# A sandwich of attention and feed-forward layers: MLPs of the state-space stage started in earlier turns, and work moved across the stage's two borders

## The chip, the core and the metric

The kernel runs on one core of one Trainium2 chip. Five engines take part: TensorE (PE, with its weight loads shown apart as PEld), VectorE (DVE), ScalarE (ACT), GpSimd (POOL) and SyncE (SP, which issues the transfers). Each engine works through its own list of instructions in the order in which the program gave them; they meet through semaphores. The metric is the device time of one execution in microseconds (us), and of several runs the median.

## The reference

Four pairs of an attention-like and a feed-forward layer work on one tensor of 16 sequences of 256 positions and 128 channels. Each layer's input is normalized, its output too, and added:

```python
x = x + _layernorm(_L2_attn_ref(_layernorm(x, axis=-1), ...), axis=-1)
x = x + _layernorm(_L2_ffn_ref(_layernorm(x, axis=-1), w1, b1, w2, b2), axis=-1)
x = x + _layernorm(_L3_attn_ref(_layernorm(x, axis=-1), ...), axis=-1)
```

The change lies in the last of these and at its two borders. `_L2_ffn_ref` is a plain MLP, `gelu(x @ w1 + b1) @ w2 + b2` with 512 hidden units. `_L3_attn_ref` is long. Cut to its skeleton, with x0 its normalized input:

```python
xm = mix_m[0] * x + mix_m[1] * x0                     # x is x0 here
n = rms_norm(xm)
value, gate = split(n @ in_proj_w)                    # value goes through a convolution of 4 taps and silu
y = selective_scan(value, A, xm @ B_proj_w, xm @ C_proj_w, dt) + D_param * value
xm = xm + mamba_scale * (y * silu(gate) @ out_proj_w)
xm = xm + m_mlp_scale * (square(relu(rms_norm(xm) @ m_fc_w)) @ m_proj_w)
xa = mix_a[0] * xm + mix_a[1] * x0                    # "the mix"
q, k, v = projections of rms_norm(xa), q and k normalized and rotated
xa = xa + attn_scale * (softmax(q k^T, causal) v @ o_w)      # 16 heads of 8
```

## The kernel before

The 4096 rows are held as eight groups (`NG`), each 512 rows: a tile of 128 partitions by 4 by 128 channels. The kernel is a sequence of stages. Each stage opens a pool of work buffers and of PSUM banks and closes them at its end, so the first tiles of a stage wait until the last instruction of the stage before it has finished with the memory.

Three stages matter here: `stage_l2_attn` (attention of the third pair), `stage_trunk` (MLP of the third pair, scan and MLP of the fourth), and `l3_gqa` (attention of the fourth pair).

Inside these stages the order of the work is written out by hand. `Ctx.turns` takes a list of generators with the turn in which each starts. In each turn it goes through the list in its order and lets each generator that has started do one step, up to its next `yield` (up to three steps if it is behind). What is issued in a turn goes to the engines' lists in that order, and no scheduler moves it afterwards.

`stage_trunk` has four kinds of generators. For each group g, `before(g)` does the whole MLP of the third pair (`l2_ffn`), then the statistics of the result, the first mix into `xm[g]`, and the values and gates of the scan (`l3_values`). `l3_scan` does the scan's 14 steps. `behind(g)` does the second MLP (`l3_mid_mlp`), and after it the mix: x is normalized again by the kept statistics, multiplied on POOL (L1685), `xm` multiplied on DVE (L1687) and the sum taken on POOL (L1688). `rotate` prepares the rotated queries and keys of group 0 for the attention. Their turns are

```python
at = [23 + 8 * g for g in range(NG)]
items = [(at[g] - 2, l3_scan(k, g, xm[g], w, lm, got[g])) for g in range(NG)]
items += [(at[g] + 12, behind(g)) for g in range(NG)]
items += [(at[g] - 23, before(g)) for g in range(NG)][::-1]
```

Thus a group enters every 8 turns; `before(g)` takes 24 turns, the scan of g starts at turn 21 + 8g and ends 14 turns later, when `behind(g)` starts.

Some buffers are few: `mlp_h`, the hidden layer, has one; `y` has two and serves the MLP's output as well as both mixes; `n` and `nT` have three.

`attention_stage` runs the two attentions. It first lets the generator `head` of group 0 do `first` steps, then calls `attention_pools`, which fills the value tiles `at_vm` and `at_pc` on POOL (L363, L368) and makes three small casts on DVE (L375), then finishes `head(0)`. This stretch lies ahead of the hand-written turns. After it, twelve turns belong to each group; heads of later groups start `early` turns ahead, and one more generator, `beside`, may be given, which starts at turn 9. In `head`, the steps up to the third make the transposed keys `kT`, the fourth the queries `qT`, the fifth `km`: `variants` (L382 on ACT and L383 on POOL) multiplies the keys by four masks, so that heads can be told apart in one product. `qm` follows likewise from the queries.

Names that a reader meets below: `k.stats` is L255 and L257 on DVE and a scaling and a power on POOL (L244, L245); `k.normed` is L264 on DVE, four instructions; L336 is the helper of every matrix product and L325 of the transposes; the scan's own DVE product is L1480; L1484 and L1485 end a half of the values; the score's maxima are L459.

Of the kernel before, what the change touches and what calls it, by code (L numbers as in the profile page):

```python
# [21 lines left out]
F32 = mybir.dt.float32  # L22
# [3 lines left out]
ALU = mybir.AluOpType  # L26
# [3 lines left out]
NB, SEQ, P, D = 16, 256, 128, 128  # L30
NG, NT, GT = 8, 4, 512
# [154 lines left out]
def idle(n):  # L186

    for _ in range(n):
        yield


def bc(ap, axis, n):

    ap = ap.unsqueeze(axis)
    shape = list(ap.shape)
    shape[axis] = n
    return ap.to_broadcast(shape)
# [1063 lines left out]
def stage_l2_attn(k, x, w, xs, decays):  # L1261

    nc, v = k.nc, k.nc.vector

    def beside():
        for g, rt in k.over.items():
            yield from soft_end(k, x[g], xs[:, g], rt, k.t([P, NT, D], "back", 1))
            yield
        yield from decays

    def head(g, got):
        yield
        if g == 0:
            xn = k.t([P, NT, D], "xn", 1)
            k.normed_act(xn, x[g], *k.kept)
            yield from idle(3)
        else:
            xn = yield from k.norm(x[g], "xn", 1, 2)
            yield
        ps = k.transposed_ps(xn)  # L1280
        xT = k.t([P, GT], "xT", 2)
        nc.scalar.copy(xT, ps)
        yield from idle(2)

        ps = k.ps("mm")
        k.mm(ps, w["wk"], xT)
        got["kT"] = k.t([P, GT], "kT", 3)
        nc.scalar.copy(got["kT"], ps)
        yield
        ps = k.ps("mm")  # L1290
        k.mm(ps, w["wq"], xT)
        got["qT"] = k.t([P, GT], "qT", 2)
        v.tensor_scalar(got["qT"], ps, 8.0**-0.5, None, ALU.mult)
        yield
        got["km"] = k.variants(got["kT"], "km")
        yield from idle(6)
        got["qm"] = k.variants(got["qT"], "qm")
        yield from idle(2)
        ps = k.tokens_ps(xT, w["wv"]).rearrange("p t (r v d) -> p t r v d", r=4, v=4)
        for n in range(4):  # L1300
            k.values_put(g, n, ps[:, :, :, n, :])
        yield

    def tail(g, yT):
        yield
        ps = k.tokens_ps(yT, w["wo"])
        y = k.t([P, NT, D], "y", 2)
        nc.scalar.copy(y, ps)
        yield
        yield from k.residual(x[g], y, 2)  # L1310

    k.attention_stage(head, 10, 4, tail, beside())


def l2_ffn(k, x, w, b2):

    v = k.nc.vector
    mv, rs = k.stats(x)
    yield
    xn = k.t([P, NT, D], "n", 3)  # L1320
    k.normed(xn, x, mv, rs)
    yield
    ps = k.transposed_ps(xn)
    xT = k.t([P, GT], "nT", 3)
    k.nc.scalar.copy(xT, ps)
    yield
    h = k.t([P, 4, GT], "mlp_h", 1)
    for n in range(4):
        ps = k.ps("s")
        k.mm(ps, w["w1"][:, n * P : (n + 1) * P], xT)  # L1330
        k.nc.scalar.activation(h[:, n, :], ps, AF.Gelu, bias=w["b1"][:, n : n + 1])
        if n % 2:
            yield
    ps = k.tokens_ps(h, w["w2"].rearrange("p (c n) -> p c n", c=4))
    yield
    y = k.t([P, NT, D], "y", 2)
    v.tensor_tensor(y, ps, bc(b2, 1, NT), ALU.add)
    yield
    mv, rs = k.stats(y)
    yield from idle(2)  # L1340
    k.normed(y, y, mv, rs)
    k.nc.gpsimd.tensor_tensor(x, x, y, ALU.add)
    yield
# [166 lines left out]
def scaled(k, w, row):  # L1510

    w = w.rearrange("p (c n) -> p c n", n=D)
    k.nc.vector.tensor_tensor(w, w, bc(row, 1, w.shape[1]), ALU.mult)
# [89 lines left out]
    return rot, vs  # L1603


def l3_gqa(k, xa, w, gain, first):

    nc, v = k.nc, k.nc.vector  # L1610

    def head(g, got):
        if g == 0:
            yield
            rot, vs = first
        else:
            rot, vs = yield from l3_rotated(k, xa[g], w)
        yield
        ps = k.transposed_ps(rot, slice(P, 2 * P))
        got["kT"] = k.t([P, GT], "kT", 3)  # L1620
        nc.scalar.copy(got["kT"], ps)
        yield
        got["qT"] = k.t([P, GT], "qT", 2)
        v.tensor_scalar(got["qT"], k.transposed_ps(rot, slice(0, P)), gain, 1.0 / math.sqrt(8.0), ALU.mult, ALU.mult)
        yield
        got["km"] = k.variants(got["kT"], "km")
        yield from idle(6)

        for t in range(NT):
            src = vs[:, t, :].rearrange("p (r d) -> p r d", r=4)  # L1630
            to = k.vm[g % 2][:, t].rearrange("p v (r n) -> p v r n", r=4)
            for u in range(2):
                nc.scalar.copy(to[:, u::2, :, 16 * u : 16 * u + 8], bc(src, 1, 2))
        yield from idle(2)
        got["qm"] = k.variants(got["qT"], "qm")
        yield

    def tail(g, yT):
        yield
        ps = k.tokens_ps(yT, w["o"])  # L1640
        y = k.t([P, NT, D], "y", 2)
        nc.scalar.copy(y, ps)
        yield
        nc.gpsimd.tensor_tensor(xa[g], xa[g], y, ALU.add)
        yield

    k.attention_stage(head, 26, 1, tail)


def stage_trunk(k, x, l2, b2, w, rows, lm, xm, first, pool):  # L1650

    nc, v = k.nc, k.nc.vector
    mix_m, mix_a = rows["resid_mix_m"], rows["resid_mix_a"]
    msum = k.t([P, D], "msum", 1)
    k.scan_val = [k.t([P, NT, 16, 32], f"scan_val{i}", 1) for i in range(2)]
    got = [{} for _ in range(NG)]

    def before(g):  # L1660
        yield from l2_ffn(k, x[g], l2, b2)
        if g == 0:
            nc.gpsimd.tensor_tensor(msum, mix_m[:, 0:D], mix_m[:, D : 2 * D], ALU.add)


        got[g]["norm"] = k.stats(x[g], f"_{g}")
        yield from idle(3)
        n0 = k.t([P, NT, D], "y", 2)
        k.normed(n0, x[g], *got[g]["norm"])
        nc.gpsimd.tensor_tensor(xm[g], n0, bc(msum, 1, NT), ALU.mult)  # L1670
        if g < 2:
            nc.gpsimd.memset(k.scan_val[g], 0.0)
        if g == 0:
            scaled(k, w["out"], rows["mamba_scale"])
            scaled(k, w["mproj"], rows["m_mlp_scale"])
            scaled(k, w["o"], rows["attn_scale"])
            scaled(k, w["aproj"], rows["a_mlp_scale"])
        yield
        yield from l3_values(k, g, xm[g], w, got[g])

    def behind(g):
        yield from l3_mid_mlp(k, xm[g], w["mfc"], w["mproj"])
        n0 = k.t([P, NT, D], "y", 2)
        k.normed(n0, x[g], *got[g]["norm"])
        nc.gpsimd.tensor_tensor(n0, n0, bc(mix_a[:, D : 2 * D], 1, NT), ALU.mult)  # L1685
        yield from idle(2)
        v.tensor_tensor(xm[g], xm[g], bc(mix_a[:, 0:D], 1, NT), ALU.mult)  # L1687
        nc.gpsimd.tensor_tensor(xm[g], xm[g], n0, ALU.add)  # L1688
        yield

    def rotate():
        first.extend((yield from l3_rotated(k, xm[0], w, 3, pool)))

    at = [23 + 8 * g for g in range(NG)]
    items = [(at[g] - 2, l3_scan(k, g, xm[g], w, lm, got[g])) for g in range(NG)]
    items += [(at[g] + 12, behind(g)) for g in range(NG)]
    items += [(at[g] - 23, before(g)) for g in range(NG)][::-1]
    with k.tc.manual_schedule():
        k.turns(items + [(at[-1] - 5, rotate())])

# [213 lines left out]
def program(ctx: ExitStack, tc: tile.TileContext, xin, dram, at, out):  # L1914
    nc = tc.nc
# [4 lines left out]
    def opened(name, side):  # L1920
        weights[name] = pool(name, side)
        return weights[name].__enter__()
# [23 lines left out]
    base = ctx.enter_context(pool("base"))  # L1946
    p0 = opened("w0", "right")
    x = [base.tile([P, NT, D], F32, tag=f"x{g}", name=f"x{g}") for g in range(NG)]
# [9 lines left out]
    k = Ctx(tc, const, None, None)  # L1958
    k.load = load
    k.mhalf = base.tile([P, P], F32, tag="mhalf", name="mhalf")  # L1960
    nc.gpsimd.memset(k.mhalf, -0.5)
    k.over = {g: base.tile([P, NT], F32, tag=f"over{g}", name=f"over{g}") for g in (NG - 2, NG - 1)}
    k.kept = [base.tile([P, NT], F32, tag=f"kept{n}", name=f"kept{n}") for n in range(2)]
    rows1 = load_rows(base, "l1rows")

# [19 lines left out]
    l2 = load(opened("wb", "right"), "l2")  # L1985
# [12 lines left out]
    l3 = load(pc, "l3", set(at["l3"]) - set(last))  # L1998
    l3.update(last)
    rows3 = load_rows(pc, "l3rows")  # L2000
# [5 lines left out]
    xm = [pm.tile([P, NT, D], F32, tag=f"xm_{g}", name=f"xm_{g}") for g in range(NG)]  # L2006
    with pool("first", "left") as pf:
        first = []
        stage("l3m", "left", stage_trunk, l2, rows1["l2b2"], l3, rows3, lm, xm, first, pf, banks=MAMBA_BANKS)
        closed("lm")  # L2010
        with phase("l3g", RING_BANKS):
            l3_gqa(k, xm, l3, l3["gain"], first)

    closed("wc")
    pd = opened("wd", "right")
# [30 lines left out]
```

## Time and profile before

| | |
|---|---|
| Median of 3 runs | 2974.41 us (2969.55 to 2975.85) |
| The profiled execution's own time | 2974.3 us |
| Its span | 2972.5 us, 59427 instructions |
| PE busy | 2756.0 us (93%), mean granted clock 0.964 |
| DVE busy | 1930.3 us (65%) |
| ACT busy | 1675.4 us (56%) |
| POOL busy | 1020.9 us (34%) |
| Scan products (L1480) | from 1908.1 to 2307.0 us |

Times inside a profile are counted from the start of the span. Busy shares are averages over stages with different limits, so what an edit is worth is to be read from the stretch in which it lies. A line of a window gives the stretch, its length, and then for each engine the busy time with the number of instructions in brackets, followed by the clock that PE was granted (1.00 is full), the share of the transfers' engines and GB/s. A line of the timeline gives the start, the duration, the engine, line and operation, `out<-in` with shapes, a count where several equal ones are merged, and in square brackets the idle time of the engine just before it with what ended it.

### The profile page before, as it was taken

The numbers are of one execution on the slowest core, as the hardware profiler recorded it, in microseconds if no ns is written. First come the engines' busy times: TensorE is split into PE (matmuls) and PEld (weight loads), VectorE is DVE, ScalarE is ACT, GpSimd is POOL, SyncE is SP. The second block draws the span as 40 slices with busy tenths as digits, with TensorE's granted clock in tenths as the row PEclk, the third lists the DMA queues.
The fourth block names the chain that finished last, engine by engine and source line by source line (L and its number), as shares of the span: only waits on it lengthen the run. The fifth ranks groups of instructions, "written<-read, shape, count | busy, mean of one in ns | idle before, by whom it ended". The sixth has DMA issues, their size and how long they took to land.

```text
span 2972.5 us, 59427 instructions
## 1 busy us (share of the span) xinstructions
PE 2756.0 (93%) x23673; PEld 1878.9 (63%) x23674; DVE 1930.3 (65%) x5300; ACT 1675.4 (56%) x3528; POOL 1020.9 (34%) x1407
## 2 busy tenths in 40 slices
PE   8889999999998799999978997899999699978998
PEld 4556766777666588888753443566666344436897
DVE  5666465564666889999866774566665577635441
ACT  6745556455565667777735665344443277756543
POOL 3553333333336100000044554323231456544332
PEclk9989999999999899999988999899999799988999
DMA  4000000000001000000020000000000000010000
GB/s 116 12 1 2 1 2 2 1 2 1 1 2 37 1 16 8 9 8 9 12 68 5 1 1 1 1 1 1 1 1 1 1 1 1 1 48 10 2 16 15
DMA packets 29149, 31.29 MB, mean 11 GB/s; under 512 B 7292, under 2 KB 20156, under 8 KB 28732
## 3 DMA queue, kind: packets, MB, share of 16 engines
q1 hardware_dynamic: 28872, 27.49, 3.1%
q8 instruction: 187, 3.06, 0.4%
q14 instruction: 90, 0.74, 0.1%
HBM read 23.29 MB, written 4.19 MB: 9 GB/s over the span
## 4 chain that ended last, share of the span: by engine, by line
PE 51%; ACT 7%; DVE 6%; POOL 2%; issue 2%; POOLq 0%; ACTq 0%; DVEq 0%
PE ps_s L336 32%; PE ps_o L336 7%; PE ps_mm L336 6%; ACT at_e L491 1%; PE ps_s L325 1%; ACT lg L1199 1%; PE ps_xin L336 1%; ACT meT L1206 1%; PE ps_sum L336 1%; ACT mdisp L1106 1%; ACT lg L1079 1%; PE ps_t L1204 1%; DVE at_nm L459 1%; PE ps_s L525 1%; POOL ln_rs L245 1%
## 5 line engine op out<-in xcount | busy, mean ns | idle before, releaser
L459 DVE TENSOR_REDUCE at_nm<-ps_s 128x2 f32<-128x512 f32 (+1 forms) x384 | 238.0, 681 | 125.1 <-PE ps_s L336 125.1
L491 ACT ACTIVATE at_e<-ps_s 128x512 f32<-128x512 f32 x384 | 198.1, 604 | 94.1 <-PE ps_s L336 91.9
L1480 DVE TENSOR_TENSOR scan<-ps_s,lm 128x384 f32<-128x384 f32 x256 | 124.6, 549 | 143.2 <-PE ps_s L336 142.9
L497 POOL TENSOR_SCALAR_AFFINE_SELECT at_e<-at_e 128x1024 f32<-128x1024 f32 (+1 forms) x96 | 135.1, 1408 | 209.5 <-ACT at_e L491 209.1
L245 POOL TENSOR_TENSOR ln_rs<-ln_rs,mhalf 128x4 f32<-128x4 f32 x192 | 196.3, 1022 | 15.2
L1015 POOL TENSOR_TENSOR ln_rs<-ln_mv,mendt 128x4 f32<-128x4 f32 x6 | 1.2, 199 | 521.2 <-DVE ln_mv L1013 521.2
L891 DVE TENSOR_REDUCE l_max<-ps_s 128x3 f32<-128x384 f32 x256 | 124.0, 548 | 61.6 <-PE ps_s L336 61.6
L336 PE MATMUL ps_o<-my,meT 128*128 128x129 f32 x1024 | 144.0, 288 | 20.9 <-ACT mgot L1218 17.1
L336 PEld LDWEIGHTS ps_s<-l_w,mlp_h 128*128 128x128 f32 x1280 | 149.5, 192 | 19.8 <-issue 15.1
L336 PE MATMUL ps_s<-l1f_phi,mxT 128*128 128x256 f32 x512 | 141.8, 401 | 21.5 <-DVE mpart L1080 15.7
L244 POOL TENSOR_SCALAR ln_rs<-ln_mv 128x4 f32<-128x4 f32 x184 | 39.6, 215 | 331.9 <-DVE ln_mv L257 312.6
L336 PEld LDWEIGHTS ps_o<-my,meT 128*128 128x128 f32 x1024 | 127.8, 195 | 39.3 <-ACT mgot L1218 22.3
L336 PE MATMUL ps_s<-km,qT 32*128 32x512 f32 x768 | 139.4, 665 | 14.0 <-POOL km L383 12.7
L336 PE MATMUL ps_s<-l_w,mlp_h 128*128 128x128 f32 x1280 | 150.4, 275 | 1.2 <-ACT mlp_h L824 0.9
L336 PE MATMUL ps_s<-qm,kT 32*128 32x512 f32 x768 | 143.0, 651 | 7.7 <-DVE at_nm L459 7.6
L941 POOL TENSOR_SCALAR_AFFINE_SELECT e<-e 128x512 f32<-128x512 f32 x128 | 78.6, 635 | 172.9 <-ACT e L938 172.9
L336 PE MATMUL ps_o<-at_e,at_vm 128*32 128x128 f32 (+1 forms) x2048 | 123.6, 338 | 15.2 <-ACT at_oT L521 15.2
L336 PE MATMUL ps_mm<-mdisp,mxn 128*128 128x128 f32 x1024 | 125.3, 279 | 5.0 <-DVE mdisp L1118 4.9
L938 ACT ACTIVATE e<-ps_s 128x384 f32<-128x384 f32 x256 | 105.5, 513 | 39.5 <-PE ps_s L336 39.4
L336 PEld LDWEIGHTS ps_mm<-mdisp,mxn 128*128 128x128 f32 x1024 | 121.8, 195 | 7.9 <-DVE mdisp L1118 6.6
L1457 ACT COPY BT<-ps_s 128x512 f32<-128x512 f32 x64 | 37.5, 586 | 154.6 <-PE ps_s L336 154.6
L336 PE MATMUL ps_s<-xT,l_w 128*128 128x512 f32 x256 | 119.7, 597 | 3.8 <-ACT mlp_h L824 2.7
(456 smaller groups left out, 7135.9 us busy)
## 6 DMA issues: line engine op xcount, KB each, us to landing
mw<-in_l1fw SPq DMA_DIRECT2D x16, 256.0 KB, 2.6
moe_w<-in_moe SPq DMA_DIRECT2D x16, 256.0 KB, 5.3
l_w<-in_l SPq DMA_DIRECT2D x10, 256.0 KB, 3.3
x<-in_x SPq DMA_DIRECT2D x8, 256.0 KB, 5.4
xs<-x SPq DMA_DIRECT2D x8, 256.0 KB, 2.1
out<-x SPq DMA_DIRECT2D x8, 256.0 KB, 2.3
slT<-xs SPq DMA_DIRECT2D x6, 256.0 KB, 2.7
l1f_phi<-in_l1f SPq DMA_DIRECT2D x1, 1024.0 KB, 5.0
```

The costliest lines, as they stand in the source:

```text
L244: g.tensor_scalar(out, in_, scale, eps, ALU.mult, ALU.add)
L245: g.tensor_tensor(out, out, self.mhalf[:, :n], ALU.pow)
L325: self.nc.tensor.transpose(out[:n, k * P : (k + 1) * P], src[:, k, cols], self.c["ident"])
L336: self.nc.tensor.matmul(out, lhsT=lhsT, rhs=rhs, start=start, stop=stop, skip_group_check=True)
L459: v_.tensor_reduce(nm[:, t, r, vs], s, AX.X, ALU.max, negate=True)
L491: nc.scalar.activation(e[:, r], s, AF.Exp)
L497: nc.gpsimd.affine_select(at, at, [[0, 4], [0, n], [1, P]], ALU.is_ge, 0.0, base=0, channel_multiplier=-1)
L891: v.tensor_reduce(mx[:, b, :, h, 16], s, AX.X, ALU.max, negate=True)
L938: nc.scalar.activation(e[:, h].rearrange("p j n -> p (j n)"), s[:, : 3 * P], AF.Exp)
L941: nc.gpsimd.affine_select(e[:, :, j, :], e[:, :, j, :], [[0, 4], [1, P]], ALU.is_ge, 0.0, base=0, channel_multiplier=-1)
L1457: nc.scalar.copy(s, ps)
L1480: v.tensor_tensor(m, s[:, : SEQ + P], lm[:, SCAN_HEADS[4 * (t // 2) + 2 * i + hh], :], ALU.mult)
```

## The change

1. While `stage_l2_attn` still runs, `tail(0)` computes the statistics of group 0's finished x and copies them on ACT into two tiles `kept2` of the base pool; `l2_ffn` of group 0 takes them from there.
2. `before(g)` starts in turn `early[g]`, which is 0, 4, 8, 16, 24, 32, 40 and 48 instead of 0, 8, ... 56, and stands idle after its MLP until the turn in which the rest of it stood before.
3. The `behind` generators stand in the list in reversed order, so the youngest group goes first within a turn.
4. The mix becomes a function `next_mix`. For the last group it is no longer done in `behind(7)`: the statistics go to `kept2` by two DVE copies, and the mix runs as the attention's `beside`.
5. `l3_gqa` lets `head(0)` do five steps instead of one ahead of `attention_pools`, so kT, qT and km are given out before the fills.

```diff
@@ stage_l2_attn, tail
         yield from k.residual(x[g], y, 2)
+        if g == 0:
+
+            yield from idle(2)
+            mv, rs = k.stats(x[g])
+            yield from idle(2)
+            nc.scalar.copy(k.kept2[0], mv)
+            nc.scalar.copy(k.kept2[1], rs)
...
-def l2_ffn(k, x, w, b2):
+def l2_ffn(k, x, w, b2, got=None):
 
     v = k.nc.vector
-    mv, rs = k.stats(x)
-    yield
+    mv, rs = got or k.stats(x)
+    if not got:
+        yield
...
-    k.attention_stage(head, 26, 1, tail)
+    k.attention_stage(head, 26, 5, tail, next_mix(k, x[NG - 1], xa[NG - 1], mix, k.kept2))
+
+
+def next_mix(k, x, xm, mix, norm):
+
+    nc = k.nc
+    n0 = k.t([P, NT, D], "y", 2)
+    k.normed(n0, x, *norm)
+    nc.gpsimd.tensor_tensor(n0, n0, bc(mix[:, D : 2 * D], 1, NT), ALU.mult)
+    yield from idle(2)
+    nc.vector.tensor_tensor(xm, xm, bc(mix[:, 0:D], 1, NT), ALU.mult)
+    nc.gpsimd.tensor_tensor(xm, xm, n0, ALU.add)
+    yield
@@ stage_trunk
     def before(g):
-        yield from l2_ffn(k, x[g], l2, b2)
+        yield from l2_ffn(k, x[g], l2, b2, k.kept2 if g == 0 else None)
+        yield from idle(at[g] - 23 - early[g])
...
     def behind(g):
         yield from l3_mid_mlp(k, xm[g], w["mfc"], w["mproj"])
-        n0 = k.t([P, NT, D], "y", 2)
-        k.normed(n0, x[g], *got[g]["norm"])
-        nc.gpsimd.tensor_tensor(n0, n0, bc(mix_a[:, D : 2 * D], 1, NT), ALU.mult)
-        yield from idle(2)
-        v.tensor_tensor(xm[g], xm[g], bc(mix_a[:, 0:D], 1, NT), ALU.mult)
-        nc.gpsimd.tensor_tensor(xm[g], xm[g], n0, ALU.add)
-        yield
+        if g == NG - 1:
+            nc.vector.tensor_copy(k.kept2[0], got[g]["norm"][0])
+            nc.vector.tensor_copy(k.kept2[1], got[g]["norm"][1])
+        else:
+            yield from next_mix(k, x[g], xm[g], mix_a, got[g]["norm"])
...
+    early = [4 * min(g, 2) + 8 * max(g - 2, 0) for g in range(NG)]
     items = [(at[g] - 2, l3_scan(k, g, xm[g], w, lm, got[g])) for g in range(NG)]
-    items += [(at[g] + 12, behind(g)) for g in range(NG)]
-    items += [(at[g] - 23, before(g)) for g in range(NG)][::-1]
+    items += [(at[g] + 12, behind(g)) for g in range(NG)][::-1]
+    items += [(early[g], before(g)) for g in range(NG)][::-1]
```

More of the change, by code (lines that the diff above doesn't have):

```diff
@@ L1603, in l3_rotated, with l3_gqa @@
     return rot, vs
-def l3_gqa(k, xa, w, gain, first):
+def l3_gqa(k, x, xa, w, gain, mix, first):
     nc, v = k.nc, k.nc.vector
@@ L1962, in program @@
     k.over = {g: base.tile([P, NT], F32, tag=f"over{g}", name=f"over{g}") for g in (NG - 2, NG - 1)}
+    k.kept2 = [base.tile(shape, F32, tag=f"kept2{n}", name=f"kept2{n}") for n, shape in enumerate(([P, NT, 2], [P, NT]))]
     k.kept = [base.tile([P, NT], F32, tag=f"kept{n}", name=f"kept{n}") for n in range(2)]
@@ L2011, in program @@
         with phase("l3g", RING_BANKS):
-            l3_gqa(k, xm, l3, l3["gain"], first)
+            l3_gqa(k, x, xm, l3, l3["gain"], rows3["resid_mix_a"], first)
     closed("wc")
```

## The prediction

> **What bounds the kernel now.** I first read the page for the place of the stage that changes. Its group `L1480 DVE ... scan` runs from 1908.1 to 2307.0 us, so `stage_trunk` is the stretch from about 1846 to 2342 us, and `l3_gqa` follows. Then I asked for the busy time of each engine in stretches that I cut at the events of that stage.
>
> ```profile
> core 0: us, PE busy (x) PEld busy (x) DVE busy (x) ACT busy (x) POOL busy (x), PEclk, DMA share, GB/s
> 1846.00:1855.00 9.00, 0.15 (x1) 0.01 (x1) 3.84 (x22) 0.59 (x1) 3.68 (x5) 0.50 0.00 1
> 1855.00:1867.00 12.00, 10.41 (x44) 6.59 (x44) 1.31 (x4) 4.62 (x6) 0.00 (x0) 0.77 0.00 1
> 1867.00:1883.00 16.00, 10.70 (x46) 6.90 (x47) 8.39 (x41) 3.33 (x5) 9.99 (x11) 0.79 0.00 0
> 1883.00:1890.90 7.90, 2.59 (x13) 1.74 (x12) 5.57 (x25) 1.17 (x2) 4.92 (x7) 0.80 0.00 0
> 1890.90:1907.10 16.20, 16.20 (x61) 9.11 (x60) 9.82 (x24) 9.81 (x17) 7.30 (x8) 0.89 0.01 2
> ...
> 1912.00:2298.00 386.00, 385.56 (x2932) 243.56 (x2930) 244.76 (x576) 169.87 (x298) 102.86 (x125) 1.00 0.00 1
> ...
> 2309.00:2342.00 33.00, 21.21 (x104) 14.41 (x104) 14.67 (x19) 12.01 (x20) 10.73 (x9) 0.84 0.01 2
> 2342.00:2353.60 11.60, 1.10 (x10) 0.87 (x10) 5.51 (x11) 4.42 (x13) 10.28 (x16) 0.63 0.00 0
> ```
>
> Read PE and its clock. In the middle, 386 us, PE is busy 385.56 us at full clock: only PE work taken out of it shortens it. At both ends PE idles, at a lowered clock: four stretches before 1890.9 leave 21 us of PE idle, and the last two leave 22 us. There the chain of waits decides. The timeline gives its two turning points.
>
> ```profile
> 1851.86 0.87 DVE L255 BATCH_NORM_STATS2 ln_st<-x 128x6 f32<-128x128 f32 x4 [1.37 <-POOL x L303]
> ...
> 1854.58 1.11 DVE L264 TENSOR_SCALAR n<-x,ln_mv,ln_rs 128x128 f32<-128x128 f32 x4 [1.56 <-POOL ln_rs L245]
> ...
> 1855.02 1.20 PE L325 MATMUL ps_s<-const_ident,n 128*128 128x128 f32 x4 [8.87 <-issue]
> ```
>
> The first instruction of the new stage waits for the last one of the old (x L303), then statistics and a power stand ahead of the first transposes.
>
> ```profile
> 2341.39 0.69 DVE L1544 TENSOR_TENSOR xm<-ps_s,xm 128x512 f32<-128x512 f32 x1 [9.34 <-PE ps_s L336]
> ...
> 2344.91 1.26 POOL L1688 TENSOR_TENSOR xm<-xm,y 128x512 f32<-128x512 f32 x1
> ...
> 2346.23 3.70 POOL L363 MEMSET at_vm<- 128x2048 f32 x2
> ...
> 2351.65 1.89 POOL L383 TENSOR_TENSOR km<-kT,const_head 128x1024 f32<-128x1024 f32 x1
> ...
> 2353.59 2.09 PE L336 MATMUL ps_s<-km,qT 32*128 32x512 f32 x8 [10.36 <-POOL km L383]
> ```
>
> The last MLP ends at 2342.08, the last mix (L1688) at 2346.17, and only then are the attention's tiles free; POOL fills them (5.4 us) and makes km after it, for which PE idles 10.36 us.
>
> [...]eight L336 `nT,l_w` took 5.38 us at 1857.0 but 3.7 us at 1894.4. [...]three small DVE casts beside the 1.88 us memset last 1.77 to 1.85 us. [...]
>
> **The change, part by part.** The order of instructions that each engine gets shows the moves: on PE one whole l2 MLP enters ahead of group 0's `xm` transposes and one leaves near the end of the steady part; SP's list, DMAs included, is the same; nothing is dropped.
>
> (1) *Statistics of group 0 taken from the attention stage* (kept2). DVE then starts with the normalization at 1851.86 instead of 1854.58: **-2.7 us**. They are paid in the attention stage as 8 DVE instructions (1.2 us), two POOL (1.2 us) and two copies on ACT of about 0.25 us (estimate from the 0.24 us of L1633). ACT queues the exponentials behind these copies, so a late POOL power would hold them; the copies come two turns later. That stage is PE-bound (98.9 us of 100 at 1700); I take +0.3, between 0 and 1.
>
> (2) *MLPs of groups 1, 2, 3 start 4, 8, 8 turns earlier.* Before the first scan there stand four MLPs instead of three. Simulating the queues by the trace's durations: MLP 0 ends on PE at 1863.6 (1866.35 less 2.7). Group 1's n was made during it, so MLP 1 follows warm: transposes 0.5, copy 0.6, four 0.86 us products with the Gelu behind, products 3.5: ends near 1872.2 (was 1883.0). MLP 2 ends near 1880.8. Group 0's own chain on DVE and POOL (bias, statistics, power 1.02, add 1.26, statistics, power, xm 2.79, memset 1.80, add for group 1 1.26, squares 1.04, power) is put behind group 1's and 2's statistics twice, some 1.2 us each, against idle DVE; `y` has two buffers, so group 2's bias waits for POOL's add of group 1, near 1881.3. Group 0's second transposes then come near 1885.1 (were 1888.37). From there the PE queue holds the same work as before, but Gelu and Silu alternate once more: two table loads, 2.56 us, and transposes of `val` stand ahead of the MLP's products. First scan near **1905.6** instead of 1907.1. So of 2.7 about 1.5 remains: parts 1 and 2 in the fill **-1.5**, from -4 to +3.
>
> (3) *One MLP fewer in the PE-bound part.* Group 7's was 0.44 us of transposes and 7.49 us of `l_w` (window 2120 to 2170): **-7.9**, from -6 (if DVE, busy 63%, shows) to -8.5. What covers nothing any more: the turns without an MLP remain full on PE (2257 to 2262).
>
> (4) *Youngest first in `behind`.* At the end `rms_ss` (L1523) of group 7 no longer waits behind 1.1 us of DVE normalization, the power not behind POOL's 1.26 us mix, and `n` of group 6 not behind 0.7 us: last transposes at 2327.1 instead of 2328.97: **-1.8**, from -0.5 to -2.5.
>
> (5) *The last mix leaves the end.* 2342.08 to 2346.23 goes, two small DVE copies (about 0.15 each) come: **-3.8**.
>
> (6) *km ahead of the fills.* One 1.88 us memset still stands first on POOL. Then km can be ready 3.8 us after release instead of 7.4, and the first scores come so much earlier. But POOL's total up to qm is unchanged, so the next group's squares (L1553) follow 9.2 us after release as before; only the DVE reduction behind them no longer waits for the first maxima (2356.26 to 2358.74). At the next wait, transposes of group 1 (2362.59), **-2.2** remains, from 0 to -3.6.
>
> (7) *The mix put back* runs at turn 9, beside group 1's keys. DVE has a gap of 1.23 us ahead of L459 at 2386.47 for the normalization, but POOL's multiplication waits for it, and km of group 1 stands behind: 2386.4 + 1.3 + 1.9 = 2389.6 instead of 2386.55. PE wants it at 2387.91: 1.6 us of stall, and the DVE product (0.68) delays maxima on a DVE that is full from 2400 to 2410. **+2.0**, from 0 to +3.5.
>
> Sum: 0.3 - 1.5 - 7.9 - 1.8 - 3.8 - 2.2 + 2.0 = **-14.9**. The profiled execution took 2974.3 us around a span of 2972.5, and the median is 2974.41; both give 2959.5.
>
> **The rivals.** *The fill was not free* (0.09): group 0's transposes wait on PE for the added MLP's full 8 us; (3) is cancelled: 2967.5. For it speaks that DVE and POOL are busy more than half in 1867 to 1891; against it, 21 us of idle PE. *The attention's start is held by something else* (0.09), DVE's casts or POOL's fills: (5), (6) give nothing, (7) costs 2: 2965.5. *Slower* (0.04): the two `y` buffers and the single `mlp_h` make the added MLP run serially ahead of group 0's values, with the 19.5 us from 1855.02 to group 0's add ending at 1874.5. The scan would begin 16.8 us late instead of 1.5 early: +18.3 - 14.9 = +3.4, 2977.8. It decides if the first scan begins after 1920. Against it: powers and adds of one MLP lie beside another's products, as before. *More than forecast* (0.10): warm PE through the fill and no stall from km: 2954. That the moves do not happen is excluded by the order.
>
> **How the numbers follow.** The likeliest case (0.68) gives 2959.5; its own bounds are about 2955 to 2965. The better case and the two smaller ones extend the range to 2952 to 2968. About 0.2% (5.9 us) is what a measurement of this kernel can tell from no change, so faster begins below 2968.5: the likeliest, the better and most of the two middle cases, 0.88; same 0.08; slower 0.04.
>
> **What would show it.** Right: first transposes near 1852.3, MLPs of groups 1 and 2 following with little PE idle, first scan before 1907, the last before 2300, the fills starting at once after the last L1544, and km second on POOL. Wrong: a first scan after 1912, turns without an MLP that keep their length by DVE, or long waits for `km` near the seventh scores.

## The result, and the profile after

The changed kernel took 2961.85 us (median of 6 runs, 2956.0 to 2966.15) beside 2975.13 us for the kernel before in the same session (6 runs, 2969.55 to 2977.73): a ratio of 0.9953, with a 95% interval of 0.9943 to 0.9963, or 13.3 us less. Its profiled execution took 2960.44 us around a span of 2958.7; against the span of 2972.5 before, that is 13.8 us less. The forecast was 2959.5, from 2952 to 2968.

The busy time of each engine in stretches, cut at events of `stage_trunk` (core 0; the first number is the length, then busy time and count for each engine, and PE's granted clock):

```profile
core 0: us, PE busy (x) PEld busy (x) DVE busy (x) ACT busy (x) POOL busy (x), PEclk, DMA share, GB/s
1857.95:1873.00 15.05, 13.02 (x54) 8.17 (x55) 6.42 (x34) 6.33 (x9) 2.60 (x5) 0.82 0.01 2
1873.00:1889.00 16.00, 13.49 (x83) 10.02 (x81) 13.18 (x39) 5.55 (x9) 11.58 (x11) 1.00 0.00 1
1889.00:1894.50 5.50, 2.21 (x6) 1.30 (x7) 3.64 (x20) 0.59 (x1) 4.12 (x6) 0.64 0.00 1
...
1918.00:2295.50 377.50, 377.30 (x2867) 237.18 (x2864) 236.97 (x549) 163.94 (x291) 95.57 (x118) 1.00 0.00 1
```

From the entry to 1894.5 PE idles 7.8 us (the first three rows). The same part of the stage before, from the entry to the second transposes of group 0:

```profile
1851.82:1890.90 39.08, 23.70 (x100) 15.24 (x101) 16.86 (x78) 9.12 (x13) 16.13 (x20) 0.76 0.00 1
```

There PE idled 15.4 us; the 21 us that the forecast read include 5.7 us ahead of the entry. The middle is as full as it was. DVE and POOL have become the busy engines of the second row: 13.18 and 11.58 of 16 us. The turning points on the timeline, where "[...]" is the wait ahead of an instruction and who ended it:

```profile
1857.95 1.11 DVE L264 TENSOR_SCALAR n<-x,kept,kept 128x128 f32<-128x128 f32 x4 [1.38 <-POOL x L303]
...
1858.40 1.20 PE L325 MATMUL ps_s<-const_ident,n 128*128 128x128 f32 x4 [6.16 <-issue]
...
2336.29 0.69 DVE L1552 TENSOR_TENSOR xm<-ps_s,xm 128x512 f32<-128x512 f32 x1 [7.07 <-PE ps_s L336]
...
2337.28 1.80 POOL L363 MEMSET at_vm<- 128x2048 f32 x1 [8.61 <-DVE kept L1706]
2339.04 1.94 POOL L383 TENSOR_TENSOR km<-kT,const_head 128x1024 f32<-128x1024 f32 x1
...
2341.87 2.09 PE L336 MATMUL ps_s<-km,qT 32*128 32x512 f32 x8 [3.73 <-DVE qT L1632]
```

The first normalization of the stage reads the kept statistics and needs nothing but `x`. POOL's fills (the memsets) start 0.30 us after the last MLP, km stands second on POOL, and PE waits 3.73 us for the first scores where it waited 10.36.

Lengths between the same events in every profiled execution, in us. Entry is the end of the last add (L303) of the second layer's attention; scans are the first and the last `scan` group of DVE (L1488, before L1480); add is the end of the last MLP's add (L1552, L1544); memset is the first one of the attention's value tiles (L363); n is L1569 (L1561) of group 1; yT is the first at_yT copy (L540) after 2400 us. Line numbers shift by a few where an edit adds or removes lines. Below, "the fill" is the stretch of the first column and "the drain" that of the third.

| kernel | entry to first scan | first to last scan | last scan to add | add to memset | memset to n | n to yT |
|---|---|---|---|---|---|---|
| before | 56.27 | 395.64 | 38.34 | 4.15 | 15.52 | 68.46 |
| changed | 55.36 | 387.77 | 35.93 | 0.30 | 13.19 | 69.88 |
| changed, again (a2) | 55.91 | 387.80 | 35.82 | 0.29 | 14.11 | 67.89 |
| e1 no early MLPs | 54.81 | 394.53 | 35.05 | 0.29 | 13.20 | 67.72 |
| e2 no kept statistics | 59.69 | 388.22 | 35.38 | 0.30 | 13.19 | 68.09 |
| e3 mix in `behind` | 55.38 | 387.79 | 35.90 | 4.15 | 13.18 | 68.76 |
| e4 fills ahead of km | 55.40 | 387.78 | 35.92 | 0.29 | 15.53 | 67.27 |
| e5 oldest first | 58.55 | 388.79 | 38.75 | 0.30 | 14.10 | 67.88 |
| e6 statistics later | 58.59 | 387.80 | 35.91 | 0.29 | 14.11 | 68.41 |
| e7 mix later | 55.39 | 387.81 | 35.91 | 0.30 | 13.19 | 68.01 |
| e8 five MLPs early | 66.08 | 381.06 | 35.81 | 0.30 | 13.19 | 68.41 |
| e9 fills early | 54.52 | 387.80 | 35.15 | 0.30 | 13.20 | 68.02 |
| e10 e6, e7 and e9 | 55.16 | 387.80 | 35.91 | 0.30 | 14.11 | 68.39 |

The 13.8 us of the two spans are not all from the change. Ahead of the first at_yT copy, at about 1615 us, where the code is the same, the changed kernel's profile is 2.8 us longer, and after the last column it is 3.9 us shorter. A2 is the changed kernel again, and there that last part is 0.2 us longer than before. Between these two points the two profiles of the changed kernel are 12.7 and 13.3 us shorter than the one before.

### The profile page after: what moved, and what is told of

Its sections match the earlier page's. It is cut to its first block, busy times and chain, and to the rows that moved or that the text cites. A ratio compares the mean times of both kernels' runs of the same rounds, so it can differ in the third digit from the quotient of the medians.

```text
span 2958.7 us, 59454 instructions
## 1 busy us (share of the span) xinstructions
PE 2757.9 (93%) x23674; PEld 1878.8 (63%) x23674; DVE 1931.3 (65%) x5302; ACT 1676.9 (57%) x3530; POOL 1017.2 (34%) x1407
## 4 chain that ended last, share of the span: by engine, by line
PE 50%; ACT 7%; DVE 7%; POOL 2%; issue 2%; DMA 0%; POOLq 0%; SPq 0%; ACTq 0%; DVEq 0%
PE ps_s L336 31%; PE ps_o L336 7%; PE ps_mm L336 6%; ACT at_e L491 1%; PE ps_s L325 1%; ACT lg L1199 1%; PE ps_xin L336 1%; ACT meT L1206 1%; PE ps_sum L336 1%; ACT mdisp L1106 1%; ACT lg L1079 1%; PE ps_t L1204 1%; DVE at_nm L459 1%; PE ps_s L525 1%; DVE scan L1488 1%
## 5 line engine op out<-in xcount | busy, mean ns | idle before, releaser
L459 DVE TENSOR_REDUCE at_nm<-ps_s 128x2 f32<-128x512 f32 (+1 forms) x384 | 238.1, 682 | 119.7 <-PE ps_s L336 119.7
L1488 DVE TENSOR_TENSOR scan<-ps_s,lm 128x384 f32<-128x384 f32 x256 | 124.7, 549 | 142.4 <-PE ps_s L336 142.2
L336 PEld LDWEIGHTS <-b_ident 128*128 128x128 bf16 x656 | 51.9, 99 | 113.1 <-issue 102.5
```

What stands on the lines that cost most here:

```text
L336: self.nc.tensor.matmul(out, lhsT=lhsT, rhs=rhs, start=start, stop=stop, skip_group_check=True)
L459: v_.tensor_reduce(nm[:, t, r, vs], s, AX.X, ALU.max, negate=True)
L1488: v.tensor_tensor(m, s[:, : SEQ + P], lm[:, SCAN_HEADS[4 * (t // 2) + 2 * i + hh], :], ALU.mult)
```

## The experiments

All but the last are the changed kernel with at most one edit, each timed at least five times; ratios are to the kernel before on the same chip. Such a ratio is known to 3 or 4 us to each side, so what an edit is worth is read from the stage lengths above and only supported by the medians.

**How far one program differs from itself (a2).** No edit.

> The changed kernel itself once more, to see how far stages of one program differ between two profiled executions. Theory, the instant at which PE gets its full clock back at a stage's border falls differently from run to run: with the same instructions the lengths from entry to first scan (55.36 us), of the drain (35.93) and from the L1569 of group 1 to the first at_yT copy after 2400 us (69.9) can differ by 1 to 3 us, the 387.77 us of scans by less than 0.1; the total within 2956 to 2966. The end of the second layer's attention took 1.6 us more than before in all seven kernels with the statistics at idle(2): theory says again. Rival, the lengths repeat within 0.1 us, and every difference between kernels is from their code.

Measured: 2961.32 us, ratio 0.9950 (0.9937 to 0.9962). The scans repeat to 0.03 us; the stages at whose start PE ran at half clock do not (in the changed kernel's first profile a granted clock of 0.50 from 1849.58 to 1863.23 us, at the start of the fill, and from 2341.10 to 2347.93, at the first scores). The first MLP's eight products, in the first profile and in this one:

```profile
1860.39 5.09 PE L336 MATMUL ps_s<-nT,l_w 128*128 128x512 f32 x8 [0.80 <-ACT nT L1333]
```
```profile
1860.48 6.76 PE L336 MATMUL ps_s<-nT,l_w 128*128 128x512 f32 x8 [0.80 <-ACT nT L1333]
```

The same instructions after the same waits, 1.67 us apart: only the instant differs at which full clock returned. In the first profile it returned at 1863.23 us, 2.84 us into the products. Eight such products take 3.70 us at a granted clock of 1.00 (at 1870.54 in the same profile); from this and the 6.76 us it returned some 6.1 us into them in a2, an estimate. In each of the 13 traces, all changes of the granted clock lie whole multiples of 3.413 us apart, and the start of the span lies anywhere from 0.3 to 3.3 us behind such an instant (0.44 in the changed kernel's first profile, 3.25 in that of the kernel before). The fill has lengths of 55.4, 55.9 and 58.6 us for one code (changed, a2, e5), at a mean granted clock of 0.89, 0.89 and 0.84, and n to yT 67.9 or 69.9. In what follows a stage is compared with runs of like mean clock ("of like clock"), or over all runs.

Memset to n, 13.2 or 14.1 us, has another cause than PE's clock. In the four profiles with 14.1 (a2, e5, e6, e10) a DVE cast takes twice as long (in a2 3.89 us for 1.90, from 2339.70 until after POOL's second memset, which runs from 2341.47 to 2343.27), qT behind it comes later, and PE waits 5.09 us for the first scores where it waited 3.73. Here the cast in a2 and then in the changed kernel's first profile:

```profile
2339.70 3.89 DVE L375 CAST b_rows<-att_rows 128x128 bf16<-128x128 f32 x1
```
```profile
2339.16 1.90 DVE L375 CAST b_rows<-att_rows 128x128 bf16<-128x128 f32 x1
```

What decides between the two is not shown, and e3 has the long cast but 13.18 us.

**MLPs at their own turns (e1).**

```diff
-    early = [4 * min(g, 2) + 8 * max(g - 2, 0) for g in range(NG)]
+    early = [at[g] - 23 for g in range(NG)]
```

> The changed kernel with the MLPs back at their own turns (early[g] = at[g] - 23); all other parts stay. Theory, PE idle time in the fill paid for nearly all of the moved MLP: first to last scan 391.0 -> 398.9 us (+7.9, one more MLP on a full PE), stage entry to first scan 55.35 -> about 53.5 (before took 56.2, less the 2.7 of the statistics, which now nothing lies ahead of), so +6 us against the changed kernel, about 2968. Rival, the fill is chain-bound and the moved MLPs cost it nothing: entry to first scan stays 55.35, +7.9. Rival, the gain came from somewhere else in the scan part: first to last scan stays near 391 and the total moves by under 2 us.

Measured: 2965.82 us, ratio 0.9969 (0.9959 to 0.9979). The scans are 6.8 us longer, the fill 0.55 shorter, the drain 0.9 shorter (not by the edit: e9, with the drain's code unedited, has 35.15 us beside 35.05): 5.3 us are lost. The moved MLP's 8 us thus cost the fill next to nothing, or up to 3.8 us where the changed kernel's fill has its slower clock (58.6 us in e5 and e6); the medians differ by 4.0. The expectation's 391.0 us count to the end of the last scan group, the table to its start. The groups of PE between first and last scan, shapes apart (count, then busy time and mean), for this kernel and for the changed one:

```profile
L336 PE MATMUL ps_s<-nT,l_w 128*128 128x512 f32 x40 | 18.8, 592 | 0.0
L336 PE MATMUL ps_s<-l_w,mlp_h 128*128 128x128 f32 x160 | 18.7, 275 | 0.0
```
```profile
L336 PE MATMUL ps_s<-nT,l_w 128*128 128x512 f32 x32 | 15.0, 592 | 0.0
L336 PE MATMUL ps_s<-l_w,mlp_h 128*128 128x128 f32 x128 | 14.9, 275 | 0.0
```

Five MLPs against four: 7.6 us of products. And why the place was free: without the early MLP, PE waits 6.27 us for group 1's `n`, and the eight products behind it take 6.69 us, against 3.70 in the changed kernel (at 1870.54, at a granted clock of 1.00).

```profile
1875.86 1.31 PE L325 MATMUL ps_s<-const_ident,n 128*128 128x128 f32 x4 [6.27 <-DVE n L264]
1877.84 6.69 PE L336 MATMUL ps_s<-nT,l_w 128*128 128x512 f32 x8 [0.68 <-ACT nT L1333]
```

**One more MLP early (e8).**

```diff
+    early = [0, 3, 6, 9] + [9 + 8 * n for n in range(1, NG - 3)]
```

> The changed kernel with one more MLP ahead of the first scan (early = 0, 3, 6, 9, 17, ... for 0, 4, 8, 16, 24, ...). It has to go through PE ahead of group 0's second transposes. Theory, a further MLP pays only for the idle time that PE has left there: the scans get 7.9 us shorter (one MLP fewer), of the 8 us in the fill 4.2 us lie in the wait for n of group 0, so entry to first scan 55.36 -> about 59.5: -3.9 in sum, about 2958. Rival, the fill is full on DVE and POOL and the MLP's statistics lengthen group 0's chain as well: +8 or more in the fill, 0 or slower. Rival, all of it is hidden: -7.9, about 2954.

Groups 1 and 2 start one and two turns earlier as well. Measured: 2960.41 us, ratio 0.9953 (0.9939 to 0.9966), the same as the changed kernel. The scans give 6.7 us; the fill takes 10.7 more than in the changed kernel's first profile and 7.5 more than in e5 and e6, whose clock there (0.84) is nearer to this one (0.86). The profiled execution took 2967.78 us, the longest of the five, so the medians, which show no difference, fit the lower figure. The wait of PE for group 0's `n` did not shrink with the added work, it grew from 4.23 to 6.43 us. The changed kernel and then this one:

```profile
1891.62 1.11 PE L325 MATMUL ps_s<-const_ident,n 128*128 128x128 f32 x4 [4.23 <-DVE n L1406]
```
```profile
1887.65 0.69 DVE L1345 TENSOR_TENSOR y<-ps_s,l1rows 128x512 f32<-128x512 f32 x1 [3.64 <-PE ps_s L336]
...
1890.75 1.11 DVE L264 TENSOR_SCALAR y<-x,ln_mv,ln_rs 128x128 f32<-128x128 f32 x4 [1.39 <-POOL x L1350]
...
1901.87 1.12 PE L325 MATMUL ps_s<-const_ident,n 128*128 128x128 f32 x4 [6.43 <-DVE n L1406]
```

The rival is right that the added MLP lengthens group 0's chain, but not by full engines: from 1873 to 1901.9 us DVE is busy 16.9 and POOL 17.6 of 28.9 us. The second line shown is group 0's normalization for its mix. In the changed kernel it stands on DVE behind the MLP bias of group 1; here it stands behind that of group 2. DVE waits 3.64 us for PE to finish that MLP and then 1.39 us more until POOL's add has freed one of the two `y` buffers.

**No statistics from the attention stage (e2).** The block `if g == 0:` in `tail` and the last argument of `l2_ffn` are gone.

> The changed kernel without the statistics of group 0 in the attention stage (they are made at the stage's start again); all else stays. Theory: POOL's pair for group 0 ahead of group 4's pair held DVE and PE, so the attention stage gets 1.65 us shorter between 1640 and 1667 us, and the wait of 2.7 us at the stage's entry comes back and is passed on to the first scan (55.35 -> about 58): +1.0 in sum, about 2963. Rival, the fill is bound by DVE and POOL behind group 0 and not by when the first transposes start: first scan at most 0.5 later after entry, and the total is 1.2 faster, about 2960.7.

Measured: 2961.26 us, ratio 0.9953 (0.9940 to 0.9965): no difference in the total, but two large ones inside. The fill is 4.3 us longer than in the changed kernel's first profile, but at a mean clock of 0.84 against 0.89; against e5 and e6, which keep the statistics and have 0.84 there too, it is 1.1 us longer. So of the 2.7 us by which the first transposes come earlier, 1.1 reach the first scan at like clock: less than the theory had and more than its rival. The attention stage ahead of it is 3.3 us shorter: in the changed kernel the at_yT copies (L540) fall back behind those of the kernel before by 1.65 us at 1672 and by another 1.6 at 1837, in this one they keep their distance throughout. In the timeline of that stage, the kernel before and then the changed one:

```profile
1656.22 1.02 POOL L245 TENSOR_TENSOR ln_rs<-ln_rs,mhalf 128x4 f32<-128x4 f32 x1
...
1657.27 2.68 DVE L264 TENSOR_SCALAR xn<-x,ln_mv,ln_rs 128x128 f32<-128x128 f32 x4 [1.05 <-POOL ln_rs L245]
```
```profile
1659.04 1.02 POOL L245 TENSOR_TENSOR ln_rs<-ln_rs,mhalf 128x4 f32<-128x4 f32 x1
...
1660.42 1.01 POOL L245 TENSOR_TENSOR ln_rs<-ln_rs,mhalf 128x4 f32<-128x4 f32 x1
...
1661.46 2.68 DVE L264 TENSOR_SCALAR xn<-x,ln_mv,ln_rs 128x128 f32<-128x128 f32 x4 [2.43 <-POOL ln_rs L245]
...
1664.80 2.48 PE L336 MATMUL ps_s<-qm,kT 32*128 32x512 f32 x7 [0.26 <-DVE at_nm L459]
```

Two powers stand in a row on POOL. The first belongs to group 0 and nobody is in a hurry for it; the second belongs to group 4, whose normalization waits on DVE, and the maxima (L459), for which PE waits, stand behind that.

**The same statistics two turns later (e6).**

```diff
-            yield from idle(2)
+            yield from idle(4)
             mv, rs = k.stats(x[g])
```

> The changed kernel with the statistics of group 0 given out two turns later in the attention stage (idle(4) for idle(2)), so that POOL's pair for group 4 stands ahead of that for group 0. Theory, the price of the statistics is the order on POOL and not their work: the 1.65 us between 1640 and 1667 us go, and the first scan keeps its distance of 55.36 us from the entry: -1.65, about 2960.2. In all four kernels with these statistics, and in neither of the two without, the end of this stage took 1.6 us more, at a lowered clock after a wait of 2.8 us: if that comes from the statistics too, it goes with them or stays, and then decides between -1.65 and -3.3. Rival, DVE and POOL are so full there that the work costs the same wherever it stands: 0.

Measured: 2960.30 us, ratio 0.9952 (0.9940 to 0.9964). The 1.65 us are gone:

```profile
1656.69 1.02 POOL L245 TENSOR_TENSOR ln_rs<-ln_rs,mhalf 128x4 f32<-128x4 f32 x1
1657.74 2.68 DVE L264 TENSOR_SCALAR xn<-x,ln_mv,ln_rs 128x128 f32<-128x128 f32 x4
...
1662.35 1.01 POOL L245 TENSOR_TENSOR ln_rs<-ln_rs,mhalf 128x4 f32<-128x4 f32 x1
```

Group 4's power now comes first and DVE does not wait. The stage's end also loses its 1.6 us. The fill of this profile was 3.2 us longer at a lower clock (0.84 for 0.89), as in e5 with unedited code there. The median is only 1.0 to 1.6 us under the changed kernel's two, so the gain of 3.3 shows in the stage alone; whether the slower fill came with the edit or by chance is not settled. That end of the stage, in the changed kernel and in e2:

```profile
1828.37 0.64 PE L336 MATMUL ps_o<-at_e,at_vm 128*32 128x256 f32 x8 [2.83 <-ACT at_oT L521]
1828.94 1.99 PE L336 MATMUL ps_s<-qm,kT 32*128 32x512 f32 x8
```
```profile
1826.41 0.64 PE L336 MATMUL ps_o<-at_e,at_vm 128*32 128x256 f32 x8 [2.82 <-ACT at_oT L521]
1826.98 1.14 PE L336 MATMUL ps_s<-qm,kT 32*128 32x512 f32 x8
```

The wait is the same to 0.01 us, but the scores behind it take 1.99 us in one and 1.14 in the other. All nine profiles with the statistics at `idle(2)` have the longer form, all four others (before, e2, e6, e10) the shorter one. What differs is where the wait lies between the instants, 3.413 us apart, on which all changes of the clock stand. Each row below reaches from one of them to the next, in the changed kernel and then in the kernel before (columns as in the first table of stretches):

```profile
1825.69:1829.10 3.41, 0.73 (x12) 0.35 (x16) 1.30 (x1) 3.05 (x7) 3.35 (x4) 1.00 0.00 0
1829.10:1832.51 3.41, 3.41 (x21) 0.85 (x22) 0.95 (x1) 1.09 (x3) 0.73 (x1) 0.50 0.00 0
```
```profile
1819.47:1822.88 3.41, 1.56 (x28) 0.52 (x20) 1.60 (x4) 3.41 (x10) 2.83 (x4) 1.00 0.00 0
1822.88:1826.29 3.41, 2.44 (x29) 0.79 (x29) 2.24 (x1) 1.77 (x4) 2.38 (x2) 1.00 0.00 0
```

In the changed kernel the wait lies almost whole within one such period, PE is busy 0.73 us of it, and the next period runs at half clock (0.50). In the kernel before, the same wait (1821.03 to 1823.85) is split by the instant at 1822.88, PE is busy 1.56 and 2.44 us, and the clock stays full (1.00). The first at_yT copy at about 1615 us lies 0.44 to 0.52 us behind such an instant in 12 of the 13 profiles, and 0.86 in e5. The 1.65 us that are lost after it carry the wait from the one place to the other, so the second loss follows from the first, as far as these 13 profiles show.

**The last mix in the feeding stage (e3).** `behind` mixes every group, and nothing runs beside the attention.

> The changed kernel with the last group's mix back in the stage that feeds the attention (all eight mixes in behind, none beside the attention; first stays 5). Theory: last MLP add to first memset 0.99 -> 4.84 us (+3.85), and the 1.4 us that km of group 1 lost behind the mix's POOL product come back: +2.45, about 2964.3. Rival, the 1.4 has another cause (group 1's chain is tight by itself after the shorter start): +3.85, about 2965.7. Rival, the memset is held by something else: no difference.

Measured: 2965.63 us, ratio 0.9967 (0.9955 to 0.9980). Add to memset is 3.85 us longer. The mix's two POOL steps stand ahead of the memset again:

```profile
2335.37 1.64 POOL L1663 TENSOR_TENSOR y<-y,l3rows 128x512 f32<-128x512 f32 x1 [9.41 <-DVE y L264]
2337.09 1.26 POOL L1666 TENSOR_TENSOR xm<-xm,y 128x512 f32<-128x512 f32 x1
...
2338.41 1.80 POOL L363 MEMSET at_vm<- 128x2048 f32 x1
```

The total moved by 3.8, not by 2.45, and n to yT, where 1.4 should have come back, stayed in its usual range: the rival is nearer, by which the mix at its new place costs nothing.

**The mix nine turns later (e7).** `yield from idle(9)` stands ahead of the mix in `l3_gqa`.

> The changed kernel with the last group's mix nine turns later in the attention stage (turn 18 for 9), where its POOL product stands behind km and qm of group 1. Theory: km of group 1 is no longer held; entry to the first at_yT copy after 2400 us gets 1.1 to 1.4 us shorter: -1.2, about 2960.6. Rival, DVE is full from 2400 to 2410 us and the mix's 1.8 us of normalization and product delay maxima there: the loss only moves, 0 to +1.

Measured: 2960.37 us, ratio 0.9951 (0.9938 to 0.9964). The changed kernel's first profile does show the stall that this edit takes away:

```profile
2376.50 1.90 POOL L383 TENSOR_TENSOR km<-kT,const_head 128x1024 f32<-128x1024 f32 x1
...
2378.45 1.10 PE L336 MATMUL ps_s<-km,qT 32*128 32x512 f32 x4 [1.26 <-POOL km L383]
```

But from n to yT the nine profiles with `first = 5` or 1 and the mix at turn 9 take 67.3 to 69.9 us (mean 68.2), the four with the mix elsewhere 68.0 to 68.8 (mean 68.4). The 69.88 of the first profile is its longest value: behind this very stall PE runs at half clock (0.50) for one period (2378.65 to 2382.06 us), which it does in none of the other eight. In the mean, the mix at turn 9 costs nothing that can be seen.

**Fills ahead of km again (e4).** `first = 1` in `l3_gqa`.

> The changed kernel with first = 1 in l3_gqa, so that POOL's fills stand ahead of km and qm again; all else stays. Theory: first scores 3.7 us later after the release, of which 2.3 reach the transposes of group 1, since PE and DVE then have work that was put between: memset to L1569 of group 1 13.19 -> 15.5 us, +2.3 in sum, about 2964.2. Rival, all of the wait for km is passed on: +3.7. Rival, the fills merely move their wait to vm (values of group 0) or to the exponentials behind them: 0.

Measured: 2963.64 us, ratio 0.9959 (0.9947 to 0.9972). Memset to n is 15.53 us, as before the change (15.52), against 13.19 in the changed kernel: +2.34.

```profile
2336.94 3.70 POOL L363 MEMSET at_vm<- 128x2048 f32 x2 [8.62 <-DVE kept L1706]
...
2342.37 1.89 POOL L383 TENSOR_TENSOR km<-kT,const_head 128x1024 f32<-128x1024 f32 x1
...
2344.31 2.09 PE L336 MATMUL ps_s<-km,qT 32*128 32x512 f32 x8 [6.51 <-POOL km L383]
```

Against the longer form, as in a2 (14.11), the same edit is worth 1.4, so 1.4 to 2.3.

**Oldest group first in `behind` (e5).** The `[::-1]` of that list is gone.

> The changed kernel with the MLPs behind the scan issued oldest group first again; all else stays. Theory: in the drain rms_ss, the power and n of the last group wait again behind work of an older group: first to last scan as it was or up to 1.1 us longer (that much of the scan's length the kernel without early MLPs was shorter than before, with only this reversal and the last mix left as reasons), last scan to the end of the last MLP add 35.9 -> about 38.3 us; +2.4 to +3.5 in sum, about 2965. Rival, the shorter drain came from the eighth group's mix that is gone (its DVE and POOL work no longer lies between) and not from the order: 0.

Measured: 2965.70 us, ratio 0.9970 (0.9958 to 0.9982). The scans are 1.0 us longer and the drain 2.8: 3.8 us. In the drain, this kernel and then the changed one:

```profile
2320.04 1.10 DVE L264 TENSOR_SCALAR y<-x,ln_mv,ln_rs 128x128 f32<-128x128 f32 x4
2321.07 0.67 DVE L1531 TENSOR_REDUCE rms_ss<-rms_sq 128x4 f32<-128x512 f32 x1
...
2324.55 1.53 DVE L1536 TENSOR_TENSOR n<-xm,rms_rs 128x512 f32<-128x512 f32 x1 [0.31 <-POOL rms_rs L245]
```
```profile
2319.75 0.68 DVE L1531 TENSOR_REDUCE rms_ss<-rms_sq 128x4 f32<-128x512 f32 x1
2320.34 1.11 DVE L264 TENSOR_SCALAR y<-x,ln_mv,ln_rs 128x128 f32<-128x128 f32 x4
...
2322.57 0.69 DVE L1536 TENSOR_TENSOR n<-xm,rms_rs 128x512 f32<-128x512 f32 x1
```

The last group's sum stands ahead of the older group's normalization or behind it, and `n` follows 3.5 or 2.8 us later. Counted from the last scan group (2300.90 here, 2301.05 in the changed kernel), `n` comes 2.1 us later: most of the 2.8. The rival by which the missing mix and not the order had shortened the drain is out, since the mix is missing here too.

**Memsets and scalings out of group 0's chain (e9).** The two memsets of `scan_val` and the four calls of `scaled` stand behind the fourth step of group 0's MLP.

> The changed kernel with the two memsets of scan_val and the four scalings of weights in the fill moved from the middle of group 0's chain (around 1881 to 1886 us) to the fifth turn, when POOL and DVE wait for the first MLP. Theory, after the change the fill is bound by group 0's chain on DVE and POOL, not by PE: n of group 0 (L1406) comes about 2.7 us earlier (DVE without 2.06 us of scalings, POOL without 1.8 us of memset[...]), the first scan about 2.5 us earlier after entry (55.36 -> 52.9), the rest unchanged: about 2959.4. Rival, PE bounds the fill with four MLPs in it: at most -0.5 at the first scan.

Measured: 2956.77 us, ratio 0.9939 (0.9927 to 0.9951). The first scan comes 0.84 us earlier, with like clock (the eight products took 5.14 and 5.09), so the mechanism is there at a third of its size. Group 0's `n` is still what PE waits for:

```profile
1861.01 3.55 POOL L1687 MEMSET scan_val<- 128x2048 f32 x2
1861.09 4.12 DVE L264 TENSOR_SCALAR n<-x,ln_mv,ln_rs 128x128 f32<-128x128 f32 x4 [1.19 <-POOL ln_rs L245]
...
1888.61 1.08 PE L325 MATMUL ps_s<-const_ident,n 128*128 128x128 f32 x4 [3.12 <-DVE n L1406]
```

Group 1's normalization of the MLP's output took 3.61 us in the changed kernel (1882.76, beside POOL's product and memset until 1885.71) and takes 2.05 here (1879.62, beside an add of 1.27). Beside the memsets now stands group 1's normalization ahead of its MLP: 4.12 us, against 1.11 in the changed kernel (1861.69), and PE does not wait for it. The median fell by 5 us; the stages of this one profile that the edit touches explain 0.8 of them, and the intervals of the two ratios overlap. The rest is open.

**Three edits together (e10).** Those of e6, e7 and e9.

> The changed kernel with the three single edits together: statistics of group 0 two turns later, the last mix nine turns later, memsets and scalings of the fill in the fifth turn. Theory, they lie in three stages and add: -1.65 in the second layer's attention (and -1.6 at its end, if that is theirs), -0.8 to -2.5 in the fill, -1.4 to -1.9 behind the third layer's first scores: -4 to -7 in sum, 2955 to 2958. Rival, what is won in one place is waited for in the next: no better than the best single one (2956.8).

Measured: 2956.11 us (5 runs, 2954.7 to 2958.25), ratio 0.9934 (0.9922 to 0.9947): the lowest of all, some 5.5 us under the changed kernel, with an interval that overlaps a little with those of its two measurements. The best single edit (e9, 2956.77) comes nearly as low, so the medians do not show that the three add. In the stages they add: in its profile 1.65 and 1.6 us are gone in the attention ahead and 0.75 in the fill (55.91 in a2, of like clock, to 55.16); behind the scores nothing.

## Why the prediction was right, and where its terms were not

The direction, the bound (PE in the middle, chains at both ends) and the sum held. Four of its seven terms were mis-sized, two of them, (1) and (4), beyond their own ranges, and they cancelled: that the sum came within 2 us is in part luck.

- **(1) Statistics in the attention stage:** forecast +0.3, found +3.3 (+1.65 by the order on POOL, +1.6 at the stage's end by the clock). The step that failed is "That stage is PE-bound" taken as a cover: it looked at ACT's exponentials for a victim and not at POOL, where group 0's scaling and power (1.2 us) were put ahead of those that another group was waiting for. E6 shows that the place and not the work was the price.
- **(1) and (2) The fill:** forecast -1.5, found -0.9 between two single profiles, within what the clock alone does to it (55.4 to 58.6 us for one code). First transposes came 2.7 us earlier as worked out, and at like clock 1.1 of them are left at the first scan (e2 against e5 and e6), where the forecast let 1.5 remain. The two table loads more that it counts are there: on ACT, between 1890 us and the first scan, loads of 1.28 us stand at 1901.17, 1903.60 and 1907.69 where the kernel before has one, at 1898.79. So the statistics, as placed, cost 3.3 us and gave 1.1.
- **(3) One MLP fewer in the middle:** forecast -7.9, found -6.8 (e1). The scans did shorten by 7.9 us, but 1.0 of it is the order in `behind` (e5). The rival "the fill was not free" fails for this MLP (0.55 us at the first profile's clock, at most 3.8) and holds for the next one (e8).
- **(4) Youngest first:** forecast -1.8, found -3.8 (e5): 2.8 in the drain (2.4 against the kernel before) and 1.0 in the scans, where the forecast had looked at the last group alone.
- **(5) The last mix leaves the end:** forecast -3.8, found -3.85 (e3).
- **(6) km ahead of fills:** forecast -2.2, found -1.4 to -2.3 (e4).
- **(7) The mix put back:** forecast +2.0, found nothing that can be seen (e3, e7). The stall on km is there (1.26 us), but in the mean it is made good before the first at_yT copies.

Found terms together, with the upper value for (6): 3.3 - 0.9 - 6.8 - 3.8 - 3.85 - 2.3 = -14.35, against -13.3 measured and -14.9 forecast. Of the marks given, the fills and km came as said. The three with a time of day did not: first transposes at 1858.4 for 1852.3, first scan products at 1912.3 for "before 1907", the last scan group at 2301.05 for "before 2300". The stage was entered 6.1 us later (3.3 from the statistics, 2.8 from the part ahead of 1615 us, whose code is the same), and by the words given, "a first scan after 1912", that would have counted as wrong although the stage itself behaved: such a mark has to be counted from an event of its own stage.

## What to carry to other kernels

Work that is moved to a stage "with room" is paid by its place in the queue of the engine that does it: look there for a short, urgent instruction of another group that it will stand ahead of, and move it a turn or two behind that one. Idle time of PE in a fill pays for added PE work only while the chain that ends the fill is not put behind that work in another engine's queue. Here one MLP was nearly free, and a second moved group 0's chain on DVE behind another group's and won nothing. Order the queue of a drain by who is last, and start what the next stage needs before what it needs later.

## What the runs showed of the hardware

PE's clock after a wait is worth as much as many an edit. One code differs from itself by 0.5 to 3.2 us in a fill of 55 us and by 2 us from n to yT, while 387.8 us of full PE repeat to 0.04 in eight profiles. The clock changed only at instants that lie whole multiples of 3.413 us apart within a trace, and at the end of the second layer's attention half clock (0.50) came or stayed away with how the wait fell between these instants. It came after a wait of 2.83 us in all nine profiles in which the wait lay almost whole within one period (in the changed kernel with 0.73 us of PE). In the four in which an instant split the same wait, the clock stayed full. How busy PE was does not decide alone: after a period with 1.56 us of PE the clock stayed full, and after the one with the stall on km, with 2.1 us, it fell.
